# Four rounds of maxima and scores in a row, two key tiles' outputs summed in one PSUM bank

## The chip, the cores and the metric

The kernel runs on one NeuronCore of a Trainium2 chip. The metric is the device time of one execution, in microseconds (us). Before the change, three runs gave a median of 4277.05 us (4273.49 to 4280.85). All arithmetic on the large operands is float32.

## The reference

A residual block over x of shape (4, 2048, 512): layer norm, self-attention with 16 heads of 32 columns whose queries and keys pass a spectral filter, and a feed-forward part in which each token goes to its best one of eight experts with 100 places each. Cut to what matters:

```python
qkv = xn @ w_qkv                              # xn: layernorm(x)
q, k, v = split into 16 heads of 32; q, k filtered by irfft(rfft(.) * mask)
scores = einsum('bhqd,bhkd->bhqk', q, k) / sqrt(32)
attn = softmax(scores, axis=-1)               # over 2048 keys
out = einsum('bhqk,bhkd->bhqd', attn, v)
return x + out @ w_out + b_out + experts(xn)
```

The attention's softmax over 2048 keys for 4 x 16 heads is most of the work.

## The kernel before

**Tiles.** Work goes by batch `b` (4), group of four heads `c` (4; `k = 4b + c` counts groups) and block `n` of 512 queries (4). A block runs over 16 tiles of 128 keys, `j`, two at a time: such a pair is a *window*, and there are 512 windows. The four heads of a group lie on the four strips of 32 partitions, so that matmuls of different heads run side by side in TensorE's array. In the trace every float32 matmul is two records.

**Two kinds of matmuls.** The stable softmax needs each query's largest score ahead of the exponentials, so scores are computed twice. `max_matmuls` multiplies queries by keys for two heads, with 128 queries on the partitions and 512 keys along the free axis; `max_reduce` takes the maxima of the two heads from PSUM by VectorE into `part`. `scores` forms the other orientation, 128 keys by 512 queries. It adds the *differences* of neighbouring key tiles (`steps_of_keys`) to the scores of the tile before, which still stand in PSUM, so a tile's scores may be written only when the exponentials of the tile before have been read there. At a block's first tile, `shift` puts the negated maxima (`negm`) into those banks. I call one `max_matmuls` with one `scores` a *round*: four matmuls, one in each strip of the array. A key tile needs two rounds (heads 0 and 1, then heads 2 and 3). The maxima of a round belong to a block some ten windows later (`MAX_AHEAD = 40` rounds ahead); the last ten windows have none left to compute.

**After the rounds.** ScalarE takes the exponentials of two heads at a time (128 x 1024) into the tile `even` or `odd`. `products` multiplies them by the values: four heads, each giving 32 rows of output and filling a quarter of the array's columns. The result is added into `num`, for a block's first tile by a ScalarE copy and otherwise by VectorE. The row sums are formed on the side: for each window POOL issues a DMA that adds `odd` into `even` (`pair`), and then POOL adds the window before (`add_to`).

**PSUM.** It has eight banks of 128 x 512 float32, all in one tile `array`. Banks 0 to 3 hold the scores of the four heads. Banks 4 to 7 are handed out in turn by `bank()` to everything else: maxima (two banks a round), a tile's outputs, and every projection.

**Order.** Each engine executes its instructions in the order of the program (`InOrder` pins them). The main loop is written out in halves of a window, one key tile each: round, round, the outputs of the tile *before* (`left`), then the side work of that half:

```python
for j in (even, odd):
    ...
    for u in range(2):
        ...
            max_matmuls(mate, mh)
        scores(k, n, j, u)
        ...
            max_reduce(mate, mh)
    ...
    if left:
        products(*left)
    ...
    for step in agenda[2 * window + (j == odd)]:
        step()
```

`agenda` is a planner's list for each half. It holds the projections of the next group (`query_key`, `value`: 48 pieces of 16 matmuls), the closing of a finished block (`close_steps`: row sums, reciprocals, four output projections `project` and a DMA that adds `y` to the output), the transposes of the next batch's normalized tokens (`turn`), and the routing to experts. `spread` places pieces so that the planned cost per half is even; `costs` tells it what a half already holds. When the maxima of a block are complete, `max_negate` reduces them on VectorE, `max_close` transposes them on TensorE, and `max_split` splits them in three bfloat16 parts on POOL and sends them by three DMAs in SP's queue to `negm`.

**Also touched.** In the stage of tokens, `bias` adds `b_out` to each x tile on POOL, and `first_sums` writes the sum to the output by SP's queue. The weights of a group's queries, keys and values arrive in one tile `wg`.

Of the kernel before, what the change touches and what calls it, by code (L numbers as in the profile page):

```python
# [25 lines left out]
P = 128  # L26
# [14 lines left out]
WIN = 2  # L41
# [62 lines left out]
def attention_and_top1_experts(ctx: ExitStack, tc: tile.TileContext, a: dict, out: bass.AP):  # L104
# [90 lines left out]
    def filter_steps(c):  # L195

        held = {}

        def turned(s):
            if s == 0:  # L200
                held["wt"] = probs(c % 2 == 1)
            pt = bank()
            for r in range(NR):
                on.tensor.transpose(
                    pt[:, r * P : (r + 1) * P], raw[s, r // 2][:, r % 2, c * P : (c + 1) * P], ident
                )
            on.vector.tensor_copy(held["wt"][:, s, 0, :], pt)

        def filtered(s):
            pw = bank()  # L210
            wt = held["wt"][:, s]
            for r in range(NR):
                at = slice(r * P, (r + 1) * P)
                on.tensor.matmul(pw[:, at], lhsT=wt[:, 0, at], rhs=filt, start=True, stop=True)
            done = pw.rearrange("p (r n) -> p r n", r=NR)
            if c == 0:
                on.scalar.copy(wg[0][:, :, s, :], done)
# [12 lines left out]
    def token_stage(b):  # L230
# [20 lines left out]
        def bias(i):  # L251
            row = held[i // TQ][:, i % TQ, :]
            on.gpsimd.tensor_tensor(row, row, b_out, ALU.add)

        def first_sums(i):

            n, t = divmod(i, TQ)
            on.sync.dma_start(out=o[b, n, :, t : t + 1, :], in_=held[n][:, t : t + 1, :])
# [149 lines left out]
        return load, measure, scale, normalize, turn, route, bias, first_sums, load_tile  # L408
# [5 lines left out]
    def load_qkv_weights(k):  # L414
        wg[k] = weights.tile([P, NR, 3, P], F32, name="wg", bufs=1)
        on.sync.dma_start(out=wg[k], in_=wd[k % NG])
# [12 lines left out]
    def query_key(k, n, s, first, last):  # L429

        here, cols = slice(first * P, last * P), slice(n * QB + first * P, n * QB + last * P)
        pq = bank()[:, here]
        for r in range(NR):
            columns(pq, wg[k][:, r, s, :], xnT[:, r, cols], start=(r == 0), stop=(r == NR - 1))
# [17 lines left out]
    def value(k, n, first, last):  # L452
        if n == 0 and first == 0:
            vs[k] = qkv.tile([P, NT, P], F32, tag="v", name="v")
        pv = bank()
        for t in range(first, last):
            i = n * TQ + t
            for r in range(NR):
                columns(
                    pv[:, t * P : (t + 1) * P],  # L460
                    xnT[:, r, i * P : (i + 1) * P],
                    wg[k][:, r, 2, :],
                    start=(r == 0),
                    stop=(r == NR - 1),
                )
# [3 lines left out]
    def projections(k, tiles=1):  # L469

        if k == 0:
            order = [(query_key, 0, 1), (query_key, 0, 0)]
            order += [(query_key, n, 1) for n in range(1, NQ)] + [(query_key, 1, 0)]
            order += [(value, n) for n in range(NQ)] + [(query_key, n, 0) for n in range(2, NQ)]
        else:
            late = [(value, n) for n in range(2, NQ)] + [(query_key, 1, 0)]
            order = [(query_key, 0, 0)] + [(value, n) for n in range(2)] + (late if k not in CROWDED else [])
            order += [(query_key, n, 1) for n in range(NQ)] + (late[::-1] if k in CROWDED else [])
            order += [(query_key, n, 0) for n in range(2, NQ)]
# [29 lines left out]
    def max_reduce(item, half):  # L509
# [3 lines left out]
        whole = joined(*half) if u == 0 else joined(*half, apart=True)  # L513
        for heads, products_of in whole:
# [37 lines left out]
    def expert_steps():  # L552


        def begin():
            w_exp = chunk("w_exp")
            on.sync.dma_start(out=w_exp, in_=a["L0_ffn_w_expert"].rearrange("(r p) n -> p r n", p=P))
            b_exp = b_out
# [111 lines left out]
    def products(k, n, j, tile, num):  # L670
        po = bank()
        four_heads(po, lambda at: vs[k][:, j, at], tile, start=True, stop=True)
        if j == 0:
            on.scalar.copy(num, po)
        else:
# [13 lines left out]
    def close_steps(k, n):  # L689
# [17 lines left out]
        def result(t):  # L707
            if t == 0:
                held["y"] = chunk("y")
            on.scalar.copy(held["y"][:, t, :], project(k, held["ot"], t))  # L710
# [29 lines left out]
    load, measure, scale, normalize, turn, first_route, first_bias, first_sums, load_tile = token_stage(0)  # L740
# [5 lines left out]
    wg[0] = weights.tile([P, NR, 3, P], F32, name="wg", bufs=1)  # L746
    nc.sync.dma_start(out=wg[0][:, :, 2, :], in_=w_qkv[:, :, 2 * DM : 2 * DM + P])
# [12 lines left out]
    nc.sync.dma_start(out=wd[0], in_=wg[0])  # L760
# [51 lines left out]
    for i, item in enumerate(stream[:MAX_AHEAD]):  # L812
# [6 lines left out]
        max_reduce(item, half)  # L819
# [12 lines left out]
    turns = itertools.cycle(range(HG, 8))  # L832
# [70 lines left out]
    def keys_from(k):  # L903

        return (9 if k in CROWDED else 6) * TQ

    def plan(k):
# [4 lines left out]
        def after_keys_are_spent(steps, start):  # L912

            first = len(steps) - keys_from(k + 1)
            for i in range(NT):
                cost, _, step = steps[first + i]
                steps[first + i] = cost, start + SPENT + i // TQ * TQ, step

        if k == 0:
            for i in range(NT):  # L920
                half = 2 + i + 5 * (i // TQ)
                at(half, load_tile, i)
                at(half + 4, first_bias, i)
                at(half + 6, first_sums, i)
# [3 lines left out]
        last = start + GH - 4  # L928
        steps = []
        if k == 0:  # L930
            done = spread([(1, 0, step) for step in first_projections], 15)
            at(done[-1] + 1, load_qkv_weights, 1)
            plan_route(20, lambda i: first_route[i]())
            ready = done[-1] + 3
        if c == NG - 2 and b + 1 < B:

            at(start + 20, begin_stage, b + 1)
            for i in range(NT):
                half = start + 20 + i + 5 * (i // TQ)
                at(half, in_stage, 8, i)  # L940
                at(half + 3, in_stage, 1, i)
                at(half + 4, in_stage, 6, i)
                at(half + 6, in_stage, 7, i)
            for n in range(NQ):
                at(start + 30 + (TQ + 5) * n, in_stage, 2, n * TQ, (n + 1) * TQ)
            for i in range(2 * TQ):
                at(start + GH - 6 + i, in_stage, 8, i)
        pieces = projections(k + 1)
        if c == NG - 1:
# [3 lines left out]
            order += pieces[4:8] + [("turn", i) for i in range(12, NT)] + pieces[8:]  # L953
            steps, first = [], start + 1
            for step in order:
                if isinstance(step, tuple):
                    i = step[1]
                    steps.append((1, start + late[i] if i in late else 0, lambda i=i: in_stage(4, i)))
                else:
                    steps.append((1, 0, step))  # L960
            steps[0] = (1, first, steps[0][2])
            after_keys_are_spent(steps, start)
# [4 lines left out]
            for i in range(2 * TQ, NT):  # L967
                at(turned[i // TQ * TQ - TQ - 1] + 1 + i % TQ, in_stage, 8, i)
            plan_route(turned[NT - 1] + 2, follow_route)
        else:  # L970
            steps = [(1, ready if k == 0 else start, step) for step in pieces]
            after_keys_are_spent(steps, start)
            done = spread(steps, last)
        assert done[-4] >= start + 3 * HB and done[-8] >= start + 2 * HB
        for i in range(NT):
            here = done[len(done) - keys_from(k + 1) + i] - start - i // TQ * TQ
            assert SPENT <= here < SPENT + 3 * TQ
        for n in range(NQ):
            at(start + GH - 10 + n * TQ, key_steps, n)
        if k + 2 < B * NG:  # L980
            at(done[-1] + 1, load_qkv_weights, k + 2)
# [13 lines left out]
    for block in range(1, B * NG * NQ):  # L995

        costs[block * HB - 4] += 0.5
# [11 lines left out]
    pairs, adds, full, splits = {}, {}, {}, {}  # L1009
    left = None  # L1010
    window = 0
    maxima = stream[MAX_AHEAD:]
    for k in range(B * NG):
        for n in range(NQ):
            num = work.tile([P, QB], F32, tag="num", name="num")
            tiles = {}
            for w in range(NW):
# [7 lines left out]
                if window in adds:  # L1025
                    add_to(*adds.pop(window))
                for j in (even, odd):
                    tiles[j] = probs(j == odd)


                    if j == 0:
                        shift(k, n)
                    for u in range(2):
                        mate = maxima.pop(0) if maxima else None
                        if mate:
                            mh = next(turns), next(turns)
                            max_matmuls(mate, mh)
# [15 lines left out]
                    for step in agenda[2 * window + (j == odd)]:  # L1053
                        step()
# [12 lines left out]
    products(*left)  # L1067
# [38 lines left out]
```

## Time and profile before

| | |
|---|---|
| median of three runs | 4277.05 us |
| the profiled execution | 4282.12 us, of which its span 4280.0 us |
| granted TensorE clock over the span | 0.993 |
| exponentials on ScalarE, 128 x 1024 | 2048 of 1021 ns |
| additions into `num` on VectorE | 960 of 677 ns |
| reciprocals on VectorE | 504 of 545 ns |
| additions of tiles on POOL, 128 x 1024 | 876 of 2524 ns |
| DMA `even<-odd`, 1 MB each | 510, 8.2 us to landing |
| first matmul on `odd` or `even` and `v` | at 107.8 us |

The busy share of an engine is the time covered by its instructions, over the span. TensorE's matmuls overlap in its pipeline and their ends are modelled, so its busy share says little of waits; the distance from one start to the next says more. A group's mean is the time of one instruction from start to end. Where the next one on the same engine starts before that end, the pace is a little shorter than the mean.

### The profile page before, as it was taken

Reading aid. Unit: us, or ns where it says so; the run is one execution under the profiler, and the core shown is the slowest. Engines: PE = TensorE matmul, PEld = TensorE weight load, DVE = VectorE, ACT = ScalarE, POOL = GpSimd, SP = SyncE. Lnnn points to the kernel's source line nnn. Section 1 sums busy time; section 2 is a strip of 40 time slices with the busy share of each in tenths; the row PEclk is TensorE's granted clock in tenths of the full one; section 3 lists DMA queues with packets and bytes.
Section 4 is the critical chain, followed back from the end, with each engine's and each line's share of the span. In section 5 each row is a group of like instructions: output and inputs, shape, how many; then the busy total and the mean of one; then the engine's idle time right before and its main releaser. Section 6 shows DMA issues by size and latency. Waiting matters only on the chain.

```text
span 4280.0 us, 120579 instructions
## 1 busy us (share of the span) xinstructions
PE 4194.3 (98%) x52270; PEld 1854.3 (43%) x52270; DVE 3411.0 (80%) x5102; ACT 2525.3 (59%) x3475; POOL 3037.6 (71%) x2110
## 2 busy tenths in 40 slices
PE   8999999999999999999999999999999999999998
PEld 4444444434444444443444444443444444444432
DVE  6767888877788888887778888887778887788885
ACT  2556655666566556557556666555755565556665
POOL 1678777876776767777677766778668776676773
PEclk9999999999999999999999999999999999999999
DMA  4767778887687778888677787888877886778788
GB/s 109 179 149 152 153 160 173 191 201 151 137 159 153 156 152 165 182 195 186 132 158 151 158 159 146 170 188 194 170 140 152 175 164 131 148 162 161 154 168 167
DMA packets 163452, 690.16 MB, mean 161 GB/s; under 512 B 27414, under 2 KB 32696, under 8 KB 97640
## 3 DMA queue, kind: packets, MB, share of 16 engines
q0 software_dynamic: 110432, 605.83, 72.1%
q1 hardware_dynamic: 51312, 76.10, 5.7%
q8 instruction: 409, 6.70, 0.6%
q14 instruction: 123, 1.01, 0.1%
q10 hardware_dynamic: 1176, 0.52, 0.1%
HBM read 59.27 MB, written 88.96 MB: 35 GB/s over the span
## 4 chain that ended last, share of the span: by engine, by line
PE 89%; DVE 6%; DMA 2%; POOL 2%; issue 1%; ACT 0%; ACTq 0%; POOLq 0%; DVEq 0%
PE array L84 89%; DVE part L84 4%; DMA even<-odd 2%; POOL even L84 1%; DVE num L84 0%; DVE stats L84 0%; DMA negm<-row 0%; DVE factor L84 0%; POOL xs L84 0%; DMA odd<-in_L_attn_w_qkv_dram 0%; DVE mv L84 0%; POOL row L84 0%; POOL rstd L84 0%; DVE even L84 0%; POOL rest L84 0%
## 5 line engine op out<-in xcount | busy, mean ns | idle before, releaser
L84 DVE TENSOR_REDUCE part<-array 128x1 f32<-128x512 f32 (+1 forms) x3336 | 2497.1, 805 | 761.6 <-PE array L84 758.3
L84 POOL TENSOR_TENSOR even<-even 128x1024 f32<-128x1024 f32 x876 | 2121.5, 2524 | 425.9 <-DMA even<-odd 417.8
L84 PE MATMUL array<-keys,q 32*128 32x512 f32 x8192 | 2089.7, 615 | 10.9 <-DVE part L84 5.5
L84 PE MATMUL array<-q,steps_of_keys 32*128 32x512 f32 x8192 | 2022.7, 618 | 3.3 <-ACT odd L84 1.7
L84 ACT ACTIVATE even<-array 128x1024 f32<-128x1024 f32 x1024 | 993.5, 1021 | 491.3 <-PE array L84 455.6
L84 ACT ACTIVATE odd<-array 128x1024 f32<-128x1024 f32 x1024 | 993.3, 1021 | 458.8 <-PE array L84 378.5
L84 PEld LDWEIGHTS array<-keys,q 32*128 32x128 f32 x8192 | 784.3, 185 | 591.3 <-DVE part L84 365.3
L84 PEld LDWEIGHTS array<-q,steps_of_keys 32*128 32x128 f32 x8192 | 707.2, 184 | 267.3 <-issue 233.1
L84 POOL DMA_DIRECT2D even<-odd x510 | 463.4, 909 | 402.2 <-ACT odd L84 321.4
L84 DVE TENSOR_TENSOR num<-num,array 128x512 f32<-128x512 f32 x960 | 650.3, 677 | 26.3 <-PE array L84 17.2
L84 PE MATMUL array<-odd,v 128*32 128x512 f32 x4096 | 549.4, 608 | 2.4 <-DVE part L84 2.4
L84 PE MATMUL array<-even,v 128*32 128x512 f32 x4096 | 547.4, 606 | 2.9 <-DVE part L84 2.9
L84 PEld LDWEIGHTS array<-xnT,wg 128*32 128x32 f32 x15808 | 439.0, 110 | 256.2 <-DVE part L84 176.2
L84 PE MATMUL array<-xnT,wg 128*32 128x128 f32 (+1 forms) x15808 | 522.0, 277 | 11.4 <-DVE part L84 10.6
L84 PEld LDWEIGHTS array<-wg,xnT 128*32 128x32 f32 x8192 | 227.9, 110 | 129.2 <-DVE part L84 94.4
L84 DVE RECIPROCAL factor<-den 128x64 f32<-128x64 f32 x504 | 274.3, 545 | 0.0
L84 PE MATMUL array<-wo,ot 128*32 128x512 f32 x2048 | 267.8, 596 | 4.0 <-POOL ot L84 4.0
L84 PE MATMUL array<-wg,xnT 128*32 128x128 f32 x8192 | 263.5, 273 | 4.4 <-DVE part L84 4.4
L84 PEld LDWEIGHTS array<-odd,v 128*32 128x32 f32 x4096 | 81.0, 108 | 394.1 <-DVE part L84 384.9
L84 PEld LDWEIGHTS array<-even,v 128*32 128x32 f32 x4096 | 80.8, 108 | 393.8 <-DVE part L84 382.7
L84 POOL DMA_DIRECT2D out_dram<-y x63 | 83.7, 1329 | 212.4 <-ACT y L84 190.9
L84 ACT COPY y<-array 128x512 f32<-128x512 f32 x252 | 147.5, 586 | 139.8 <-PE array L84 139.4
(129 smaller groups left out, 1490.5 us busy)
## 6 DMA issues: line engine op xcount, KB each, us to landing
even<-odd POOLq DMA_DIRECT2D x510, 1024.0 KB, 8.2
out_dram<-y POOLq DMA_DIRECT2D x63, 1024.0 KB, 10.1
xs<-in_L_attn_x_dram SPq DMA_DIRECT2D x112, 256.0 KB
out_dram<-xs SPq DMA_DIRECT2D x64, 256.0 KB
wg<-wd SPq DMA_DIRECT2D x15, 768.0 KB
wo<-in_L_attn_w_out_dram SPq DMA_DIRECT2D x16, 256.0 KB
negm<-row SPq DMA_DIRECT2D x192, 4.0 KB
xs<-in_L_attn_x_dram SPq DMA_DIRECT2D x2, 1024.0 KB
```

Of the source, the lines that this page charges most:

```text
L84: done = act(*args, **kwargs)
```

## The change

Each window now has this order on TensorE: `shift` at a block's first window, four rounds (two for the even key tile, two for the odd one), the outputs of the even tile, the side work of both halves, and the outputs of the odd tile. Outputs are no longer put off by a half.

Both tiles' outputs are summed in one bank `po`: the even tile's matmuls have `start` set, the odd tile's `stop`, and `num` takes the sum once for each window. The banks 4 to 7 are split in two pairs, `near` and `far`. Rounds 1 and 3 write their maxima to `near`, rounds 2 and 4 to `far`; `po` is the first bank of `near`, and the side work takes turns in the three others. After each window the pairs change places. All maxima of a round are reduced by one instruction over two banks; before, the first round of a tile had one for each head.

`max_close` stands between the two halves of side work, in the window in which the maxima became complete, and `max_split` at the head of the next window.

Beside that: the projections of a group have another order, and the weights of queries, keys and values have a tile and a load of their own (`w0`, `w1`, `w2`). The output begins as a copy of x, from DRAM to DRAM, and `b_out` is added to `y` by VectorE for the first group of each batch; `bias` and its loads of x tiles for the first batch are gone. The planner counts a transpose of tokens as half a piece.

```diff
-    def max_reduce(item, half):
+    def max_reduce(item, half, apart=True):
...
-        whole = joined(*half) if u == 0 else joined(*half, apart=True)
-        for heads, products_of in whole:
+        for heads, products_of in joined(*half, apart):
...
-    def products(k, n, j, tile, num):
-        po = bank()
-        four_heads(po, lambda at: vs[k][:, j, at], tile, start=True, stop=True)
-        if j == 0:
+    def products(k, n, j, tile, po, num):
+
+        odd = j % WIN == WIN - 1
+        four_heads(po, lambda at: vs[k][:, j, at], tile, start=not odd, stop=odd)
+        if j == WIN - 1:
             on.scalar.copy(num, po)
-        else:
+        elif odd:
             on.vector.tensor_tensor(num, num, po, ALU.add)
...
-            on.scalar.copy(held["y"][:, t, :], project(k, held["ot"], t))
+            if k % NG == 0:
+                on.vector.tensor_tensor(held["y"][:, t, :], project(k, held["ot"], t), b_out, ALU.add)
+            else:
+                on.scalar.copy(held["y"][:, t, :], project(k, held["ot"], t))
...
-    turns = itertools.cycle(range(HG, 8))
+    near, far = (4, 5), (6, 7)
...
-        costs[block * HB - 4] += 0.5
+        costs[block * HB - 6] += 0.25
...
                 for j in (even, odd):
                     tiles[j] = probs(j == odd)
-
-
-                    if j == 0:
-                        shift(k, n)
                     for u in range(2):
                         mate = maxima.pop(0) if maxima else None
                         if mate:
-                            mh = next(turns), next(turns)
-                            max_matmuls(mate, mh)
+                            banks = far if u else near
+                            max_matmuls(mate, banks)
                         scores(k, n, j, u)
                         both = array[:, 2 * u : 2 * u + 2, :]
                         on.scalar.activation(tiles[j][:, u], both, AF.Exp, scale=SCALE)
                         if mate:
-                            max_reduce(mate, mh)
-                    while full_blocks:
-                        filled = full_blocks.pop(0)
-                        max_negate(*filled)
-                        full[window + 1] = filled
-                    if left:
-                        products(*left)
-                    left = k, n, j, tiles[j], num
-                    if j == even and window in full:
-                        splits[window + 1] = full.pop(window)
-                        max_close(*splits[window + 1])
-                    for step in agenda[2 * window + (j == odd)]:
-                        step()
+                            max_reduce(mate, banks, False)
+                for filled in full_blocks:
+                    max_negate(*filled)
+                po = array[:, near[0], :]
+                turns = itertools.cycle((near[1], *far))
+                products(k, n, even, tiles[even], po, num)
+                for step in agenda[2 * window]:
+                    step()
+                while full_blocks:
+                    splits[window + 1] = full_blocks.pop(0)
+                    max_close(*splits[window + 1])
+                for step in agenda[2 * window + 1]:
+                    step()
+                products(k, n, odd, tiles[odd], po, num)
+                near, far = far, near
```

More of the change, by code (lines that the diff above doesn't have):

```diff
@@ L216, in filtered @@
             if c == 0:
-                on.scalar.copy(wg[0][:, :, s, :], done)
+                on.scalar.copy(wg[0, s], done)
             else:
@@ L249, in measure, with first_sums @@
             on.vector.bn_aggr(mv[:, i, :], stats[:, i, :])
[L251 to L258, printed above, removed]
+        def first_sums(n):
+            on.sync.dma_start(out=o[b, n], in_=x[b, n])
         def scale(first=0, last=NT, shift_on=None):
@@ L407, in token_stage, with load_qkv_weights @@
         route += [lambda i=i: enter(i) for i in range(NT)]
-        return load, measure, scale, normalize, turn, route, bias, first_sums, load_tile
+        return load, measure, scale, normalize, turn, route, first_sums, load_tile
     qs, vs = {}, {}
     wo = {}
-    def load_qkv_weights(k):
-        wg[k] = weights.tile([P, NR, 3, P], F32, name="wg", bufs=1)
-        on.sync.dma_start(out=wg[k], in_=wd[k % NG])
+    def load_qkv_weights(k, s):
+        wg[k, s] = weights.tile([P, NR, P], F32, name=f"w{s}", bufs=1)
+        on.sync.dma_start(out=wg[k, s], in_=wd[k % NG][:, :, s, :])
     def load_out_weights(k):
@@ L433, in query_key @@
         for r in range(NR):
-            columns(pq, wg[k][:, r, s, :], xnT[:, r, cols], start=(r == 0), stop=(r == NR - 1))
+            columns(pq, wg[k, s][:, r, :], xnT[:, r, cols], start=(r == 0), stop=(r == NR - 1))
         if s == 0:
@@ L461, in value @@
                     xnT[:, r, i * P : (i + 1) * P],
-                    wg[k][:, r, 2, :],
+                    wg[k, 2][:, r, :],
                     start=(r == 0),
@@ L467, in value, with projections @@
         on.scalar.copy(vs[k][:, n * TQ + first : n * TQ + last, :], done)
-    def projections(k, tiles=1):
+    def projections(k, tiles=1, kinds=None):
+        kinds = [] if kinds is None else kinds
         if k == 0:
@@ L475, in projections @@
         else:
[L476 to L479, printed above, removed]
+            first = 2 if k in CROWDED else 3 if k % NG == 0 else 4
+            queries, vals = ([(f, n, *s) for n in range(NQ)] for f, *s in ((query_key, 0), (value,)))
+            news = [(query_key, n, 1) for n in range(NQ)]
+            if first == 4:
+                order = vals + queries[:2] + news + queries[2:]
+            else:
+                order = vals[:first] + queries[:1] + news[:3]
+                order += vals[first : first + 1] + news[3:] + vals[first + 1 :] + queries[1:]
+        kinds.extend((2 if f is value else at[1]) for f, *at in order for t in range(0, TQ, tiles))
         return [
@@ L557, in begin @@
             on.sync.dma_start(out=w_exp, in_=a["L0_ffn_w_expert"].rearrange("(r p) n -> p r n", p=P))
-            b_exp = b_out
+            b_exp = work.tile([P, DM], F32, tag="b_exp", name="b_exp", bufs=1)
             on.sync.dma_start(out=b_exp, in_=a["L0_ffn_b_expert"].partition_broadcast(P))
@@ L709, in result @@
                 held["y"] = chunk("y")
-            on.scalar.copy(held["y"][:, t, :], project(k, held["ot"], t))
+            if k % NG == 0:
+                on.vector.tensor_tensor(held["y"][:, t, :], project(k, held["ot"], t), b_out, ALU.add)
+            else:
+                on.scalar.copy(held["y"][:, t, :], project(k, held["ot"], t))
         def add():
@@ L737, in close_last @@
                 on.sync.dma_start(out=o[b, n, :, t - 1 : t + 1, :], in_=y[:, t - 1 : t + 1, :])
-    load, measure, scale, normalize, turn, first_route, first_bias, first_sums, load_tile = token_stage(0)
+    load, measure, scale, normalize, turn, first_route, first_sums, _ = token_stage(0)
     load(0)
@@ L745, in attention_and_top1_experts @@
     load(3, probs(False).rearrange("p u h q -> p (u h) q"))
-    wg[0] = weights.tile([P, NR, 3, P], F32, name="wg", bufs=1)
-    nc.sync.dma_start(out=wg[0][:, :, 2, :], in_=w_qkv[:, :, 2 * DM : 2 * DM + P])
+    for s in range(3):
+        wg[0, s] = weights.tile([P, NR, P], F32, name=f"w{s}", bufs=1)
+    nc.sync.dma_start(out=wg[0, 2], in_=w_qkv[:, :, 2 * DM : 2 * DM + P])
     for c in range(1, NG):
@@ L759, in attention_and_top1_experts @@
             measure(i - 2 * NG + TQ)
-    nc.sync.dma_start(out=wd[0], in_=wg[0])
+    for s in range(3):
+        nc.sync.dma_start(out=wd[0][:, :, s, :], in_=wg[0, s])
     first_projections = projections(0, TQ)
@@ L818, in attention_and_top1_experts @@
         max_matmuls(item, half)
-        max_reduce(item, half)
+        max_reduce(item, half, False)
         if i in ahead:
@@ L901, in place_experts @@
                 free += 2
-    def keys_from(k):
-        return (9 if k in CROWDED else 6) * TQ
     def plan(k):
@@ L910, in plan, with after_keys_are_spent @@
         start = k * GH
[L912 to L917, printed above, removed]
-        if k == 0:
[L920 to L924, printed above, removed]
+        def after_keys_are_spent():
+            for i, place in enumerate([j for j, s in enumerate(kinds) if s == 1]):
+                cost, _, step = steps[place]
+                steps[place] = cost, start + SPENT + i // TQ * TQ, step
+        if k == 0:
+            for n in range(NQ):
+                at(2 + (TQ + 5) * n, first_sums, n)
         if k + 1 == B * NG:
@@ L927, in plan @@
         at(start + GH // 2, load_out_weights, k + 1)
-        last = start + GH - 4
-        steps = []
+        last = start + GH - 1
+        steps, kinds = [], []
         if k == 0:
             done = spread([(1, 0, step) for step in first_projections], 15)
-            at(done[-1] + 1, load_qkv_weights, 1)
+            for s in range(3):
+                at(done[-1] + 1, load_qkv_weights, 1, s)
             plan_route(20, lambda i: first_route[i]())
@@ L938, in plan @@
             for i in range(NT):
[L939 to L945, printed above, removed]
+                half = start + 2 * HB - 2 + i + 8 * (i // (NT // 2))
+                at(half - 4, in_stage, 7, i)
+                at(half, in_stage, 1, i)
+                if i % TQ == TQ - 1:
+                    n = i // TQ
+                    at(half + 1, in_stage, 2, n * TQ, (n + 1) * TQ)
+                    at(half - 2, in_stage, 6, n)
             for i in range(2 * TQ):
-                at(start + GH - 6 + i, in_stage, 8, i)
-        pieces = projections(k + 1)
+                at(start + GH - 6 + i, in_stage, 7, i)
+        pieces = projections(k + 1, kinds=kinds)
         if c == NG - 1:
@@ L953, in plan @@
             order += pieces[4:8] + [("turn", i) for i in range(12, NT)] + pieces[8:]
+            kinds = [None] * 8 + kinds[:4] + [None] * 4 + kinds[4:8] + [None] * 4 + kinds[8:]
             steps, first = [], start + 1
@@ L957, in plan @@
                     i = step[1]
-                    steps.append((1, start + late[i] if i in late else 0, lambda i=i: in_stage(4, i)))
+                    steps.append((0.5, start + late[i] if i in late else 0, lambda i=i: in_stage(4, i)))
                 else:
                     steps.append((1, 0, step))
-            steps[0] = (1, first, steps[0][2])
-            after_keys_are_spent(steps, start)
+            steps[0] = (0.5, first, steps[0][2])
+            after_keys_are_spent()
             done = spread(steps, last)
@@ L967, in plan @@
             for i in range(2 * TQ, NT):
-                at(turned[i // TQ * TQ - TQ - 1] + 1 + i % TQ, in_stage, 8, i)
+                at(turned[i // TQ * TQ - TQ - 1] + 1 + i % TQ, in_stage, 7, i)
             plan_route(turned[NT - 1] + 2, follow_route)
@@ L971, in plan @@
             steps = [(1, ready if k == 0 else start, step) for step in pieces]
-            after_keys_are_spent(steps, start)
+            after_keys_are_spent()
             done = spread(steps, last)
         assert done[-4] >= start + 3 * HB and done[-8] >= start + 2 * HB
-        for i in range(NT):
-            here = done[len(done) - keys_from(k + 1) + i] - start - i // TQ * TQ
-            assert SPENT <= here < SPENT + 3 * TQ
+        places = [[h for h, s in zip(done, kinds) if s == kind] for kind in range(3)]
+        for i, h in enumerate(places[1]):
+            assert SPENT <= h - start - i // TQ * TQ < SPENT + 3 * TQ
+        assert places[0][3] < start + GH - MAX_AHEAD // 2 and places[0][7] < start + GH + HB - MAX_AHEAD // 2
         for n in range(NQ):
@@ L980, in plan @@
         if k + 2 < B * NG:
-            at(done[-1] + 1, load_qkv_weights, k + 2)
+            for s in range(3):
+                at(places[s][-1] + 1, load_qkv_weights, k + 2, s)
     SPENT = GH - HB - MAX_AHEAD // 2 + TQ
@@ L1007, in add_to @@
             engine.tensor_tensor(tile[:, u], tile[:, u], sum_before[:, u], ALU.add)
-    pairs, adds, full, splits = {}, {}, {}, {}
-    left = None
+    pairs, adds, splits = {}, {}, {}
     window = 0
@@ L1026, in attention_and_top1_experts @@
                     add_to(*adds.pop(window))
+                if even == 0:
+                    shift(k, n)
                 for j in (even, odd):
                     tiles[j] = probs(j == odd)
-                    if j == 0:
-                        shift(k, n)
                     for u in range(2):
@@ L1066, in attention_and_top1_experts @@
             ended[k, n] = num, tiles[NT - WIN]
-    products(*left)
+    turns = itertools.cycle(range(8))
     add_to(*adds.pop(window))
```

## The prediction

> **What bounds the kernel now.** I read the page's busy shares first, then its chain of waits, then the groups by shape, the list of waits, and last the timeline of single halves. The first two name TensorE:
>
> ```profile
> PE 4194.3 (98%) x52270; PEld 1854.3 (43%) x52270; DVE 3411.0 (80%) x5102; ACT 2525.3 (59%) x3475; POOL 3037.6 (71%) x2110
> ...
> PE array L84 89%; DVE part L84 4%; DMA even<-odd 2%; POOL even L84 1%; DVE num L84 0%; DVE stats L84 0%; DMA negm<-row 0%; DVE factor L84 0%; POOL xs L84 0%; DMA odd<-in_L_attn_w_qkv_dram 0%; DVE mv L84 0%; POOL row L84 0%; POOL rstd L84 0%; DVE even L84 0%; POOL rest L84 0%
> ```
>
> PE carries 89% of the chain, and the only other piece of weight is VectorE's maxima (`part`), 4%. So the question is what the change does to PE's sequence and where VectorE could make PE wait. The groups by shape give the prices of a maximum, of one head (512 columns) and of two heads in one instruction (1024):
>
> ```profile
> L84 DVE TENSOR_REDUCE part<-array 128x1 f32<-128x512 f32 x2576 | 1633.2, 683 | 745.8 <-PE array L84 742.8
> ...
> L84 DVE TENSOR_REDUCE part<-array 128x2 f32<-128x1024 f32 x760 | 925.0, 1217 | 15.8 <-PE array L84 15.6
> ```
>
> Now a common half of before, PE's timeline (start, length):
>
> ```profile
> 158.69 0.70 PE L84 MATMUL array<-keys,q 32*128 32x512 f32 x2
> ...
> 160.62 1.07 PE L84 MATMUL array<-odd,v 128*32 128x512 f32 x8
> 161.51 1.06 PE L84 MATMUL array<-xnT,wg 128*32 128x128 f32 x32
> 162.49 0.70 PE L84 MATMUL array<-keys,q 32*128 32x512 f32 x2
> ```
>
> Two rounds take 1.93 us, one tile's outputs 0.89, one projection 0.98, in all 3.80. Then two halves without side work, where a wait appears (brackets: idle before, and who ended it):
>
> ```profile
> 287.01 0.70 PE L84 MATMUL array<-keys,q 32*128 32x512 f32 x2
> 287.99 0.59 PE L84 MATMUL array<-keys,q 32*128 32x512 f32 x2
> 288.17 2.42 DVE L84 TENSOR_REDUCE part<-array 128x1 f32<-128x512 f32 x3 [1.20 <-PE array L84]
> 288.33 1.94 ACT L84 ACTIVATE even<-array 128x1024 f32<-128x1024 f32 x2 [0.92 <-PE array L84]
> 288.42 0.59 PE L84 MATMUL array<-keys,q 32*128 32x512 f32 x2
> 288.94 1.06 PE L84 MATMUL array<-odd,v 128*32 128x512 f32 x8
> 289.94 1.40 PE L84 MATMUL array<-keys,q 32*128 32x512 f32 x3
> 290.51 0.68 DVE L84 TENSOR_TENSOR num<-num,array 128x512 f32<-128x512 f32 x1
> 290.65 0.18 PEld L84 LDWEIGHTS array<-keys,q 32*128 32x128 f32 x1 [0.42 <-DVE part L84]
> 292.57 1.06 PE L84 MATMUL array<-even,v 128*32 128x512 f32 x8
> ```
>
> The reader should see five things. (1) A round is two passes of four concurrent heads; an inner pass takes 0.43 (287.99 to 288.42), so a round is 0.86. Entering the round phase costs 0.11 more (287.01 to 287.99 is 0.98), leaving it 0.1 (288.42 to 288.94 is 0.52). (2) Outputs followed by rounds take 1.00, followed by a projection 0.89: the return costs another 0.11. (3) VectorE starts on a round's maxima 1.16 after the round began, ScalarE on its exponentials at 1.32. (4) In the second half the previous half's maxima are not finished: PE stands from about 290 until 290.65 and the round phase takes 2.63 (289.94 to 292.57). One output and no side work is too little to cover VectorE. (5) After that wait PE needs 1.92 for the two rounds, as from a fresh start.
>
> VectorE's pace in a row:
>
> ```profile
> 2448.77 2.42 DVE L84 TENSOR_REDUCE part<-array 128x1 f32<-128x512 f32 x3 [0.16 <-PE array L84]
> 2451.10 0.68 DVE L84 TENSOR_TENSOR num<-num,array 128x512 f32<-128x512 f32 x1
> ```
>
> Two singles at 0.60 and a double of 1.22 make 2.42; the next instruction starts 0.09 before the double ends. So a double is 1.13 start to start, 1.22 to its end. In the half above the double thus ended at 290.60 and PE resumed at 290.65: 0.05 for the release.
>
> **The change, part by part.**
>
> *Four rounds in a row, on two pairs of banks.* Rounds 1 and 3 put maxima in `near`, rounds 2 and 4 in `far`; all maxima are now doubles. Round 3 cannot write before VectorE has read round 1, nor round 4 before round 2, and `po` is `near[0]`, so the outputs wait for round 3's maximum. Count from PE's first round:
> - round 1 at 0, round 2 at 0.98; maximum 1 from 1.16 to 2.38 (VectorE free at 2.29).
> - round 3 at 2.43 (unhindered: 1.84). Maximum 2 from 2.29 to 3.51.
> - round 4 at 3.56 (round 3 itself, as a fresh start of 0.98, is over at 3.41). Maximum 3 needs round 3: 2.43 + 1.16 = 3.59, to 4.81.
> - outputs at 4.86 (PE alone: 3.56 + 0.98 + 0.1 = 4.64). Maximum 4 from 4.72 to 5.94.
>
> ScalarE (1.02 an exponential, 0.97 in a row) ends number 1 at 2.34 and number 2 at 3.3, before the maxima do. Behind round 3's waiting matmul stand its own scores, then all of PE; so nothing covers the wait. I add 0.02 for the weights that can't load ahead of the outputs: **4.88 a window**, where two round phases were 3.86. Bounds: 4.69 if VectorE loses nothing waiting for round 3 (1.16 + 2 x 1.13 + 1.22 + 0.05), 5.0 if each restart exposes another 0.1 of weight loading. I take 4.88, since the half at 289.94 shows a restart that costs a fresh start and no more.
>
> *Switches between rounds and outputs.* [...] Before has two phases of each shape in a window, after has one. [...] Entry and exit are inside the 4.88; only the return is booked apart.
>
> *Sum over 512 windows.* Before: 1024 round phases at 1.93 are 1976 us; adding up what single ones took above that gives 69 (137 of them, like the second half above); 1024 returns at 0.11 are 113; together 2158. After: 512 x 4.88 = 2499, plus 512 returns, 56: 2555. **Difference +397.** Of the 69 nothing stays, as the 4.88 holds VectorE's whole lateness.
>
> *Closing of a block's maxima.* Before, `max_close` (a transpose by PE) stands in the half after `max_negate`, behind products: its halves take 4.65 where 4.1 would do. After, steps and an output lie between: about -30 over 63 blocks (bounds 0 and -35). The split of the negated maxima comes a window earlier; four blocks of before wait 5.5 to 6.5 us for `negm`, whose transfers stand behind others in SP's queue. One more window (over 8 us) covers them: -24 (bounds 0 and -24).
>
> *Output sums.* 448 fewer additions into `num` on VectorE at 0.60, 268 us. They lie where VectorE waits for PE: nothing. The remaining one ends 0.9 after the last output, before round 2 needs that bank.
>
> *b_out on `y` by VectorE* (64 additions of 0.68), *no `bias` on POOL* (64 of 1.55), *64 fewer tile loads, `out<-x` DRAM to DRAM, weights in three tiles, reordered projections:* all beside PE; the side work's matmuls are the same in number. POOL has 5.9 us of work in an 8.2 us window and gets longer windows. SP's queue gets 16 transfers of 1 MB ahead of `negm`; if one landed late it would cost at most the 6.5 us above, each. Prologue doubles: -2. Windows without side work wait 0.2 for the odd exponential (5.9): 27 of them, +5. The last ten windows have no maxima; there the exponentials (1.32 + 1.02 before round 3, 2.24 + 1.02 before round 4) hold the phase at about 4.3, which I leave in the 4.88 (-5 at most).
>
> Sum: 397 - 30 - 24 + 3 = +346 on the profiled 4282.1 (span 4280.0): 4628; the median of before lies 5 lower, so **4623 us**, 8% slower.
>
> **Rivals.**
> *A, slower as worked out: 0.84.* Its range, from the round phase alone, is 4526 (4.69) to 4685 (5.0), and -0 / +54 for the two closing terms.
> *B, faster: 0.06.* The four rounds run at PE's pace, 0.98 + 0.86 + 0.86 + 0.95 = 3.65. Then 512 x 3.65 + 56 = 1925 against 2158: -233, with the closing terms about 3995. It decides from a round phase below 4.2 (2158 + 54 - 56 over 512). For it: VectorE is only 80% busy and loses work. Against: this needs a 1024-column maximum in half the 1.22 us that 760 rows show.
> *C, much slower: 0.06.* PE's pauses cost it the clock. [...] If the outputs ran at half clock, 0.86 a window: 5060.
> *D, no difference: 0.01*, the closing point of B by chance. The remaining 0.03 is A with `negm` or tile sums late in most windows, above 4750.
>
> **Numbers.** The range 4510 to 4725 takes in A's bounds. A run of this kernel can tell 0.2% (9 us) from no change. Faster 0.06, within 0.2% 0.01, slower 0.93.
>
> **What would show it.** Right: a gap on PE before the third and fourth rounds and before the outputs, each released by `part`; windows with two projections near 8.5 us instead of 7.6; PE below 90% busy; VectorE busy less in total yet a far larger share of the chain; 2048 doubles and no singles. Wrong: rounds 0.86 apart all through, or PE waiting for `even`, `odd` or `negm` instead.

## The result, and the profile after

The changed kernel takes 4648.33 us (median of 4 runs, 4648.11 to 4649.77); the kernel before, on the same chip, 4277.45. The ratio is 1.0868, with a 95% interval of 1.0849 to 1.0887: slower by 371 us. The profiled execution has a span of 4646.3 us at a granted clock of 0.998.

From the page of the changed kernel, the busy shares, the chain of waits by line, and the costliest group:

```profile
PE 4270.5 (92%) x52270; PEld 1706.2 (37%) x52270; DVE 3103.7 (67%) x3375; ACT 2546.2 (55%) x3411; POOL 2968.0 (64%) x2046
...
PE array L84 70%; DVE part L84 27%; ACT even L84 0%; ACT xs L84 0%; DVE stats L84 0%; ACT xnT L84 0%; ACT odd L84 0%; DMA odd<-in_L_attn_w_qkv_dram 0%; POOL rstd L84 0%; DMA mask<-_L_attn_mask_logits_dram 0%; DVE factor L84 0%; DVE xs L84 0%; DVE mv L84 0%; ACT y L84 0%; DVE shift L84 0%
...
L84 DVE TENSOR_REDUCE part<-array 128x2 f32<-128x1024 f32 (+1 forms) x2057 | 2414.4, 1216 | 434.7 <-PE array L84 384.7
...
L84 PE MATMUL array<-keys,q 32*128 32x512 f32 x8192 | 2170.3, 628 | 238.7 <-DVE part L84 234.3
```

The last line's group in the kernel before:

```profile
L84 PE MATMUL array<-keys,q 32*128 32x512 f32 x8192 | 2089.7, 615 | 10.9 <-DVE part L84 5.5 <-ACT q L84 4.9
```

VectorE's busy time fell by 307 us, from 80 to 67% of the span, yet its share of the chain rose from 4 to 27%. PE now stands idle in front of new maxima until VectorE has read the bank (239 us before these matmuls; 11 us before the change). With the outputs' waits, the list of waits has 1001 such gaps of PE, 329 us in all. VectorE's lower busy share says nothing of slack here; what counts is that PE waits for the maxima of three of the four rounds in a window like the one below.

One window of the changed kernel, from its timeline (start, length; in brackets the idle time before and who ended it):

```profile
2002.96 0.70 PE L84 MATMUL array<-keys,q 32*128 32x512 f32 x2
...
2003.94 1.05 PE L84 MATMUL array<-keys,q 32*128 32x512 f32 x4
...
2004.16 4.81 DVE L84 TENSOR_REDUCE part<-array 128x2 f32<-128x1024 f32 x4 [0.35 <-PE array L84]
2004.28 1.94 ACT L84 ACTIVATE even<-array 128x1024 f32<-128x1024 f32 x2 [1.76 <-PE array L84]
...
2005.44 0.70 PE L84 MATMUL array<-keys,q 32*128 32x512 f32 x2 [0.44 <-DVE part L84]
...
2005.97 0.59 PE L84 MATMUL array<-keys,q 32*128 32x512 f32 x2
...
2006.57 0.19 PEld L84 LDWEIGHTS array<-keys,q 32*128 32x128 f32 x2 [0.82 <-DVE part L84]
...
2007.90 1.07 PE L84 MATMUL array<-even,v 128*32 128x512 f32 x8 [0.18 <-DVE part L84]
...
2008.78 2.80 PE L84 MATMUL array<-xnT,w 128*32 128x128 f32 x96
```

Rounds 1 to 4 start at 0, 0.98, 2.48 and 3.61, the outputs at 4.94. VectorE's four doubles run from 1.20 to 6.01 (merged in one line of 4.81, which hides a pause of 0.1 before round 3's), and each of PE's three late starts is released by `part`. Afterwards VectorE has nearly nothing to do for the 2.8 us of side work, which would have been the cover. Over the trace, the median of 502 such phases is 4.94 us.

### The profile page after: what moved, and what is told of

Same layout as the page of the kernel before. It is cut to its first block, busy times and chain, and to the rows that moved or that the text cites. A ratio compares the mean times of both kernels' runs of the same rounds, so it can differ in the third digit from the quotient of the medians.

```text
span 4646.3 us, 117998 instructions
## 1 busy us (share of the span) xinstructions
PE 4270.5 (92%) x52270; PEld 1706.2 (37%) x52270; DVE 3103.7 (67%) x3375; ACT 2546.2 (55%) x3411; POOL 2968.0 (64%) x2046
## 4 chain that ended last, share of the span: by engine, by line
PE 70%; DVE 27%; issue 2%; ACT 1%; DMA 0%; POOL 0%; ACTq 0%; DVEq 0%; POOLq 0%
PE array L84 70%; DVE part L84 27%; ACT even L84 0%; ACT xs L84 0%; DVE stats L84 0%; ACT xnT L84 0%; ACT odd L84 0%; DMA odd<-in_L_attn_w_qkv_dram 0%; POOL rstd L84 0%; DMA mask<-_L_attn_mask_logits_dram 0%; DVE factor L84 0%; DVE xs L84 0%; DVE mv L84 0%; ACT y L84 0%; DVE shift L84 0%
## 5 line engine op out<-in xcount | busy, mean ns | idle before, releaser
L84 DVE TENSOR_REDUCE part<-array 128x2 f32<-128x1024 f32 (+1 forms) x2057 | 2414.4, 1216 | 434.7 <-PE array L84 384.7
L84 PE MATMUL array<-keys,q 32*128 32x512 f32 x8192 | 2170.3, 628 | 238.7 <-DVE part L84 234.3
L84 PE MATMUL array<-q,steps_of_keys 32*128 32x512 f32 x8192 | 2167.4, 630 | 11.3 <-ACT even L84 11.3
L84 PEld LDWEIGHTS array<-keys,q 32*128 32x128 f32 x8192 | 626.6, 183 | 1728.2 <-DVE part L84 1067.2
L84 DVE TENSOR_TENSOR num<-num,array 128x512 f32<-128x512 f32 x448 | 308.1, 688 | 958.3 <-PE array L84 946.1
L84 PEld LDWEIGHTS array<-q,steps_of_keys 32*128 32x128 f32 x8192 | 621.8, 183 | 36.0 <-ACT even L84 26.2
L84 PEld LDWEIGHTS array<-xnT,w 128*32 128x32 f32 x15808 | 446.2, 110 | 155.3 <-issue 149.6
L84 PE MATMUL array<-xnT,w 128*32 128x128 f32 (+1 forms) x15808 | 501.8, 277 | 0.7 <-ACT xnT L84 0.7
L84 PEld LDWEIGHTS array<-w,xnT 128*32 128x32 f32 x8192 | 230.6, 110 | 86.3 <-issue 82.2
L84 PE MATMUL array<-w,xnT 128*32 128x128 f32 x8192 | 255.4, 273 | 0.0
```

Source lines behind the costliest of these rows:

```text
L84: done = act(*args, **kwargs)
```

## The experiments

The first four change the new kernel and look for what holds the four rounds. They ran on one chip beside the kernel before, 4281.46 us there. Each is a single execution, as is the next (`b1_doubles`), and the changed kernel was not run beside them: its 4648 us are from the chip on which the kernel before took 4277.45. So differences of some 4 us from it mean nothing. Kernels that leave out part of the work serve for timing only.

**Half the maximum (`e1_half_max`).** VectorE reads half of each bank:

```diff
-            on.vector.reduce_max(part[:, heads], products_of, axis=AX.X)
+            on.vector.reduce_max(part[:, heads], products_of[:, :, 0 : QB // 2], axis=AX.X)
```

> The changed kernel, but VectorE takes each maximum over the first 256 of 512 key columns (part of the computation is left out); banks, order and waits are the same. Theory (VectorE's maxima on two pairs of banks pace the four rounds): a maximum falls from 1.22 to about 0.65 us, round 3 no longer waits for it, and the next wait behind it decides, ScalarE's exponentials (number 1 over at 1.32 + 1.02, number 2 at 3.3): the round phase falls from 4.94 to 4.3 or 4.4 us, the time from 4648 to about 4350. Rival (the loss is in TensorE's own new order, or VectorE alone was the limit): 4648 in the first case; 3.65 a phase and about 4000 in the second.

Measured: 4343.31 us, phase 4.34 (median), as the theory had it. The maxima take 0.69 us. The timeline of this kernel shows the next wait:

```profile
2504.10 0.70 PE L84 MATMUL array<-keys,q 32*128 32x512 f32 x2
...
2505.39 1.94 ACT L84 ACTIVATE even<-array 128x1024 f32<-128x1024 f32 x2 [3.70 <-PE array L84]
...
2506.02 0.70 PE L84 MATMUL array<-keys,q 32*128 32x512 f32 x2
...
2506.47 0.70 PE L84 MATMUL array<-q,steps_of_keys 32*128 32x512 f32 x2
...
2507.38 0.19 PEld L84 LDWEIGHTS array<-q,steps_of_keys 32*128 32x128 f32 x2 [0.19 <-ACT even L84]
```

Round 3's maxima now start at 1.92, but its scores only at 2.37, 0.06 after the first exponential (1.29 + 1.02) ends; round 4's scores wait for the second one. So about 305 us of the changed kernel's time were VectorE's, and ScalarE stood right behind. Even so the kernel is slower than before: maxima of 0.69 us in place of 1.22 would not have made this order pay.

**Half the exponentials (`e2_half_exp`).** The core of the edit, beside which POOL's and the DMA's sums take the same half:

```diff
-                        both = array[:, 2 * u : 2 * u + 2, :]
-                        on.scalar.activation(tiles[j][:, u], both, AF.Exp, scale=SCALE)
+                        both = array[:, 2 * u : 2 * u + 2, 0:HQ]
+                        on.scalar.activation(tiles[j][:, u, :, 0:HQ], both, AF.Exp, scale=SCALE)
...
-            on.tensor.matmul(out[at], lhsT=weights(at), rhs=pr[:, h // 2, h % 2, :], **flags)
+            twice = pr[:, h // 2, h % 2 : h % 2 + 1, 0:HQ].to_broadcast([P, 2, HQ])
+            on.tensor.matmul(out[at].rearrange("p (a q) -> p a q", a=2), lhsT=weights(at), rhs=twice, **flags)
```

> The changed kernel, but ScalarE takes exponentials of only the first 256 of 512 queries of each head, and the outputs and row sums read these columns twice (the other half of the tiles is left out, in the DMA and POOL sums too); TensorE's work is the same. Theory: the exponentials are ready before the maxima are, so the time stays at 4648 to within 0.5% (4625 to 4670). Rival (ScalarE paces the rounds): the phase falls by half a microsecond, 4400 or less.

Measured: 4631.37 us, within the theory's limits, and the phase unchanged at 4.94. Half of the 17 us come from the last ten windows, which have no maxima: their phase falls from 4.22 to 3.37. ScalarE at 37% busy in place of 55% buys nothing while VectorE is the later of the two; the sums of half the size on POOL (48% busy) do not either, so POOL and its DMAs are not in this.

**Both halves (`e3_half_both`).**

> Both edits at once: maxima over 256 columns and exponentials of 256 queries (both halves left out). Theory: neither engine is late, TensorE runs the four rounds at its own pace, 3.65 to 3.75 us a phase, and the time is about 4025 (4000 to 4080); this is what one change of shape in place of two would be worth if nothing had to be emptied from PSUM. Rival (something else, such as reading the weights of waiting matmuls or a bank written while its neighbour is read, holds the phase): above 4250.

Measured: 4106.03 us, phase 3.90. That is the theory's side, but outside its numbers (4080 and 3.75 at most). Rounds in this kernel's timeline:

```profile
2002.48 0.70 PE L85 MATMUL array<-keys,q 32*128 32x512 f32 x2
...
2003.46 1.03 PE L85 MATMUL array<-keys,q 32*128 32x512 f32 x4
...
2003.68 0.69 DVE L85 TENSOR_REDUCE part<-array 128x2 f32<-128x512 f32 x1 [0.38 <-PE array L85]
...
2004.43 0.70 PE L85 MATMUL array<-keys,q 32*128 32x512 f32 x2
...
2004.96 0.59 PE L85 MATMUL array<-keys,q 32*128 32x512 f32 x2
2004.97 1.02 PE L85 MATMUL array<-q,steps_of_keys 32*128 32x512 f32 x4
2005.40 0.59 PE L85 MATMUL array<-keys,q 32*128 32x512 f32 x2
...
2006.36 1.06 PE L85 MATMUL array<-even,v 128*32 128x512 f32 x8
```

Round 3 comes at 1.95, since even a maximum of 0.69 ends at 1.89; unhindered it would have come at 1.84. And its first pass takes 0.53 (2004.43 to 2004.96) in place of 0.43, though it follows rounds of its own shape. So here a wait of 0.1 costs 0.2. The four cases together, time and phase in us:

| | exponentials whole | exponentials half |
|---|---|---|
| maxima whole | 4648, 4.94 | 4631, 4.94 |
| maxima half | 4343, 4.34 | 4106, 3.90 |

The two phases of before take 2 x 1.93 = 3.86. So with half of both engines' work left out the phase is still no shorter than before. What this case gains on the kernel before (175 us) is about what other terms give: 69 us of late maxima, 57 of returns, and 57 of the change's other parts (shown below), less 20 for the phase.

**Singles in rounds 1 and 3 (`e4_singles`).**

```diff
-                            max_reduce(mate, banks, False)
+                            max_reduce(mate, banks, u == 0)
```

> The changed kernel with the maxima of rounds 1 and 3 taken by one instruction for each head, as the first round of a tile was before; rounds 2 and 4 stay doubles. Theory: the outputs' bank is free after the first single of round 3, so they wait only for TensorE's own round 4; round 4 itself comes 0.1 later: phase 4.75 in place of 4.94, time about 4555. Rival (a shorter queue of VectorE is worth more than an early bank): 4.94 + 0.17, about 4730.

Measured: 4531.47 us, phase 4.70 (4555 and 4.75 expected): 117 us less than the changed kernel with 1004 more instructions on VectorE, all work done. The timeline of this kernel:

```profile
2003.33 0.70 PE L84 MATMUL array<-keys,q 32*128 32x512 f32 x2
...
2004.49 4.88 DVE L84 TENSOR_REDUCE part<-array 128x1 f32<-128x512 f32 x6 [0.33 <-PE array L84]
...
2005.83 0.18 PEld L84 LDWEIGHTS array<-keys,q 32*128 32x128 f32 x1 [0.30 <-DVE part L84]
...
2006.96 0.70 PE L84 MATMUL array<-keys,q 32*128 32x512 f32 x2
...
2008.03 0.16 PEld L84 LDWEIGHTS array<-even,v 128*32 128x32 f32 x8 [0.76 <-DVE part L84]
```

The outputs start 1.07 after round 4, PE's own time for a restarted round with the change of shape. (The line names `part`, but the same 0.76 stands before outputs that no maximum holds up, as at 288.94 in the kernel before.) A short queue matters less here than the moment at which the first bank is given back.

**Doubles in the kernel before (`b1_doubles`),** on another chip, beside 4278.98 us:

```diff
-        whole = joined(*half) if u == 0 else joined(*half, apart=True)
+        whole = joined(*half)
```

> The kernel before with one edit: all maxima of two neighbouring banks are doubles, in the first round of a tile too. Theory: there the outputs take the first bank of round 1, which a single frees at 1.8 us, before TensorE wants it at 1.93, but a double frees at 2.43; half a microsecond in about three quarters of 1024 halves (where round 1 has neighbouring banks): about 4650. Rival (fewer and cheaper instructions on VectorE help or cost nothing): 4230 to 4280.

Measured: 4579.11 us. One flag costs 300 us: the theory's mechanism, but 70 us less than its sum. The timeline of this kernel:

```profile
2003.22 0.70 PE L84 MATMUL array<-keys,q 32*128 32x512 f32 x2
...
2004.39 2.42 DVE L84 TENSOR_REDUCE part<-array 128x2 f32<-128x1024 f32 x3 [1.38 <-PE array L84]
...
2005.67 1.06 PE L84 MATMUL array<-odd,v 128*32 128x512 f32 x8 [0.46 <-DVE part L84]
```

The outputs start at 2.45 in place of 1.93, right behind the double (1.17 + 1.22 + 0.05). What round phases took above 1.93 us rises from 66 to 419 us over 1004 of them. That is 353, of which 300 show in the time. Much of the other 53 can be read from the traces: with longer rounds PE no longer waits for `negm` (26.7 us of waits before, none here), and the 44 halves with one projection and a closing take 14 us less in all behind their rounds.

**The old loop in the changed kernel (`a1_old_loop`)** leaves everything of the change but the loop, with 5 rounds of timing on a third chip, as the next:

```diff
-                            banks = far if u else near
-                            max_matmuls(mate, banks)
+                            mh = next(turns), next(turns)
+                            max_matmuls(mate, mh)
...
+                    if left:
+                        products(*left)
+                    left = k, n, j, tiles[j], num
+                    for step in agenda[2 * window + (j == odd)]:
+                        step()
```

> The changed kernel with the old loop alone put back: two rounds, the outputs of the tile before, side work, for each half; maxima of a tile's first round as singles; banks in turn; each tile's outputs added to num. Everything else of the change stays (order of projections, weights in three tiles, output begun as a copy of x, b_out on y, closing behind side work). Theory: the whole loss is in the loop, and the rest is worth what the closing is: 4200 to 4250 us. Rival (the other parts cost time too): above 4290.

Measured: 4224.79 us (4224.16 to 4229.24) against 4282.03 before; ratio 0.9867, interval 0.9852 to 0.9882. This version beats both kernels: 57 us under the kernel before, 423 under the changed one (428 if each is taken against the kernel before on its own chip). The loop alone costs those 423 to 428. No run takes the sum of two tiles in one bank apart from the order of the rounds, so their shares of it stay open.

**The closing alone (`b2_close`).** In the kernel before, beside the same 4282.03 us:

```diff
-                    if j == even and window in full:
-                        splits[window + 1] = full.pop(window)
-                        max_close(*splits[window + 1])
                     for step in agenda[2 * window + (j == odd)]:
                         step()
+                    while full_blocks:
+                        splits[window + 1] = full_blocks.pop(0)
+                        max_close(*splits[window + 1])
```

> The kernel before, with max_close behind the side work of the half in which a block's maxima are complete, and so max_split a window earlier. Theory: the 0.54 us that 44 halves with a closing lose to the next projection's bank, and the 24 us of four blocks that wait for negm, go: 4277 - 28 - 24, about 4225 us. Rival (the closing was hidden, or its cost moves to the next half): 4270 to 4285.

Measured: 4268.89 us, ratio 0.9971 (0.9960 to 0.9981): 13 us, a miss. The mechanism is there: halves with one projection and a closing take 4.21 us in place of 4.65 (the closing now stands one half earlier), and no wait for `negm` is left. But most is given back: round phases longer than 1.98 us rise from 137 to 196, and their excess from 66 to 86 us. The trace shows why. Around one closing:

```profile
1457.17 0.39 PE L84 MATMUL array<-square,neg 128*16 128x128 f32 x2
1457.50 0.97 PE L84 MATMUL array<-keys,q 32*128 32x512 f32 x2
...
1457.77 0.25 ACT L84 COPY rest<-array 16x128 f32<-16x128 f32 x1
...
1458.03 0.86 PE L84 MATMUL array<-keys,q 32*128 32x512 f32 x2
```

The transpose now stands right before a round, and part of that round's maxima starts only at 1458.03, when ScalarE has read the transposed bank (1457.77 + 0.25). This phase takes 2.29 in place of 1.93. Taken with the half behind it, 63 closings bring 4 us. The waits for `negm` fell away, but at three of the four places PE then waits elsewhere: at the first, two halves (from 882 us in the kernel before) take 7.8 us less, and the five behind them 5.8 more. POOL's row sums are late in these stretches: over the whole trace ScalarE waits 52.6 us for POOL's `even`, 30.2 before, and TensorE's row sums about 6, which they did not before.

The kernel before also lost clock at these waits, which its mean of 0.993 hides:

```profile
891.50:898.00 6.50, 5.34 (x28) 1.65 (x28) 2.51 (x3) 2.05 (x2) 6.50 (x5) 0.51 0.88 208
```

This row covers the stretch behind the wait that ends at 892.66; 0.51 is the granted clock. The other three waits are followed by 0.50 to 0.54; at the first three places `b2_close` shows 1.00. The half of a window behind each wait takes 5.15, 5.44, 5.11 and 3.74 us, and 2.89, 2.88, 2.91 and 2.31 in `b2_close`. So the four waits took 24 us, and the clock behind them 8 more.

**The rest of the gain (`a2_bias`, `a3_plan`).** Each takes the version of 4225 us and puts one group of parts back, beside 4280.37 us before. Cores of the edits:

```diff
-            for n in range(NQ):
-                at(2 + (TQ + 5) * n, first_sums, n)
+            for i in range(NT):
+                half = 2 + i + 5 * (i // TQ)
+                at(half, load_tile, i)
+                at(half + 4, first_bias, i)
+                at(half + 6, first_sums, i)
```

```diff
-        last = start + GH - 1
+        last = start + GH - 4
...
-        costs[block * HB - 6] += 0.25
+        costs[block * HB - 4] += 0.5
```

> The changed kernel with the old loop (4225 us), and with the old way to begin the output put back as well: x tiles loaded, b_out added by POOL, the sums written by SP's queue at the old places, y copied by ScalarE. If the stage of tokens was what the rest of the change gained by, 4255 to 4270 us; if the planner was, 4220 to 4235.

> The changed kernel with the old loop (4225 us), and with the old planning put back: the old order of projections, their last half three earlier, a token transpose counted as a whole piece, the old allowance at a block's end. If the planner was the gain, through halves that it leaves without side work (83 before, 45 with the new planning), 4250 to 4270 us; if the stage of tokens was, 4220 to 4235.

Measured: 4249.91 us and 4241.07 us (ratios to before 0.9928 and 0.9907, intervals 0.9914 to 0.9941 and 0.9892 to 0.9922). Neither is the whole: the stage of tokens is worth 25 us, the planning 16. With the 13 of the closing this makes 54 of the 57, if such shares add up. The planning's count fits: 90 halves without side work with the old one, 45 with the new. What `a2_bias` loses stands nearly all in the three stretches in which the next batch's tokens are prepared (from 824, 1849 and 2874 us, some 125 us each): PE's row sums wait 7.4 us there for POOL's `even`, and none do in `a1_old_loop`. These are the places at which `b2_close` gave its gain back.

## Why the prediction was right, point by point

**The round phase.** Predicted 4.88, measured 4.94, and its bounds of 4.69 and 5.0 held. The chain of causes is the one worked out: maxima on two pairs of banks, PE in order, the outputs behind round 3's maximum. The difference is mainly one term, VectorE's start after a round, taken as 1.16: it is 1.20 behind round 1 and 1.18 behind round 3 (medians). Each of the two maxima is with its release 0.01 longer. That makes 0.08, less the 0.02 put on for weights. The 0.06 over 502 phases are 30 us. The 0.02 was the author's estimate, and no run shows it: in `b1_doubles` the outputs start 0.06 behind the end of the double (2005.61 and 2005.67), where the release alone took 0.05 in the kernel before. That the whole sum fell short by 25, nearly as much, needed the luck told below.

**The wait behind the wait.** The working had ScalarE ready just ahead of VectorE, and the last ten windows at about 4.3 (measured 4.22). Yet rival B set the whole gain against VectorE alone: a maximum in half the time was to give a phase of 3.65 and about 3995 us. `e1` shows 4.34 and 4343. For B both engines would have had to be twice as fast, and more.

**Switches.** One phase of each shape less would save an entry, an exit and a return: 0.11 + 0.1 + 0.11 = 0.32 us a window by the rows of (1) and (2), 164 us in 512 windows. That estimate did not hold while anything waited: PE pays about 0.1 at a restart too, as round 3 of `e3` shows (0.53 in place of 0.43). Of the three terms the working kept only the return as a gain, and counted each restart in the 4.88 as a fresh start; so the sum was right here.

**Closing and `negm`.** Booked at -54, the waits for `negm` did vanish from the changed kernel, and its windows with two projections and a closing take 8.78 against 8.54 without, which leaves room for a transpose and no stall. Alone they brought 13 us in the kernel before. The clock that the waits cost, 8 us, was not booked: it can't be seen in the page's clock row, whose 40 slices are 107 us long and all show nine tenths.

**Costed at nothing.** Here two steps were wrong. The stage of tokens (POOL's `bias`, tile loads, the output's start) and the planning were called beside PE; with the old loop they are worth 25 and 16 us, 41 together. The closing with `negm` was booked 41 too high, as far as its 13 us in the kernel before measure it. So all off the loop, booked at -51, measures -57, but as the sum of other parts than those named: that these errors cancel is luck. The loop, booked at +397, measures +423 to +428.

**What would show it.** Windows with two projections took 8.50 and 8.54 (predicted 8.5; the first are output projections), the share of `part` in the chain rose as expected, and maxima are doubles but for a few of the prologue. PE's busy share is 92%, where below 90 was expected; the modelled ends of matmuls may cover part of the waits, which no run here can show. Rival C, a lost clock, did not come: 0.998 granted, more than the 0.993 before.

The emptying of PSUM decided here: VectorE needs 1.14 us from one maximum to the next, and PE 0.86 for a round that waits for nothing. What a change of shape costs by itself is not settled: first passes behind one are 0.1 us longer (round 1 of the window above takes 0.98 in place of 0.86), but so are those behind a wait without one (0.53 in place of 0.43 in round 3 of `e3`).

## What to carry to other kernels

Before putting like with like to save changes of shape, write down for each round when its banks are given back, engine by engine, and how much other work lies between two uses of them. In this kernel a consumer that is slower than the producer (1.14 us for two banks, against 0.86) needs that work *between* the bursts; its low busy share over the whole span (67%) is no sign of slack. And the wait behind the first wait sets how much a faster consumer could bring at all: here 305 us with VectorE alone, 542 with ScalarE too (`e1`, `e3`).

## What the runs showed that was not expected

The extra 0.1 us of a first pass is no property of the change of shape alone: rounds 3 and 4 of the changed kernel pay it after their waits, and round 3 of `e3` after one of 0.1 us behind matmuls of the same shape (0.53 against 0.43 each time). Joining two maxima in one instruction shortens VectorE's queue by 0.06 us (two singles take 1.20 from start to start, a double 1.14) and holds the first bank about 0.5 us longer (1.22 in place of 0.68); in the kernel before that cost 300 us, in the changed one 117. And a wait was worth less than its length: without the first one for `negm` two halves take 7.8 us less, and the five behind them 5.8 more. POOL seems to have caught up with the row sums while PE waited (it was busy for 14.35 of the 15 us from 885 to 900 in the kernel before).
